# A graph-attention kernel's edge-list stage: two halves of a row searched as one, a mask by a square, and an order written by hand

## The chip, the cores and the metric

The kernel runs on one core of one Trainium2 chip. The metric is device time in microseconds of one execution. Five engines work side by side, each through its own queue in order: PE (matmul), DVE (vector), ACT (scalar, activations), POOL (GpSimd) and SP (which only issues DMAs here). They wait for each other through semaphores.

## The reference

4096 nodes carry 512 features each; `adj` is a 4096 x 4096 integer matrix, on average sparse, with denser rows and columns at low indices. The expected degree of row n and column j falls as 1/sqrt((n+1)(j+1)). Three attention layers run over the same edges, then two dense layers:

```python
h = jnp.einsum('nf,kfp->knp', node_matrix, W)
e = jax.nn.leaky_relu(f2[:, :, None] + f1[:, None, :], negative_slope=0.2)
e = jnp.where(adjacency_matrix[None, :, :] > 0, e, NEG_INF)
out = jnp.einsum('knm,kmp->knp', jax.nn.softmax(e, axis=-1), h)
...
x = _layernorm(x + layer0(x, adj))      # 8 heads of 64
x = _layernorm(x + layer1(x, adj))      # 8 heads, then 1 head of 512, then 512 -> 1024 -> 512
```

A row without edges takes the mean over all nodes. What matters here is that the edges of each row must be found once, as a list of source indices.

## The kernel before, in words

The kernel has a sparse path, whose result is used when all bounds of the lists hold, and a dense one, which is not entered with these inputs. The sparse path has a **graph stage** (`find_edges`, with `edge_constants` and `signs_of`), two head layers, and a last layer with the dense part. The head layers gather rows of a table of projected features by indirect DMA (L1094) with the lists of the graph stage. The change touches the graph stage and the functions beside it.

The graph stage goes through 32 tiles of 128 rows. Tile 0, the densest, is cut into four parts by columns; every other tile is one part, so that there are 35 parts (class `Part`). For a part:

- SP loads 128 x 4096 integers of `adj` (L846), ACT turns them into signs in bf16 (L848).
- **Keys.** For each 512 columns PE adds, in PSUM, the sign through an identity (L878) and a number that grows with the column (L879, `places` by `frac`). A column without an edge has a key below 1, a column with an edge 1 plus its place. Two windows of 1024 columns fit (`pk`, two buffers).
- **Maxima.** DVE takes the eight largest keys of each segment (`nc.vector.max`, L885). Segments are cut so that more than eight edges in one are very unlikely; tile 0 takes three rounds each, with `match_replace` (L888). The results lie side by side in `cand`.
- **List rounds.** DVE takes the k largest of `cand`, eight at a time (L900, L902), into `lst`.
- **Counts.** ACT turns the keys into column numbers `qs` (L907) and counts edges (L910); POOL makes the row's count (L912 to L929).
- **Place.** PE forms prefix sums over the rows (L933, `prs`); ACT reads them three times (L934, L939, L940), makes two Sign maps over the slots of the part (L944, L945), and POOL adds them (L946) into a matrix `s1` that says which slot belongs to which row. PE spreads the lists over slots (`pl`, L962 to L971, one buffer in PSUM), ACT copies the owner row of each slot (L973), DVE selects the one right entry of each slot (L979 to L983, or L988 for long lists), and POOL writes the index (L994 to L996).

`place` of a part is written into the program one part behind its maxima. Beside the parts, `beside(t)` projects tile t of x for the first layer: a load, four transposes on PE, eight small instructions on ACT (L686), eight matmuls (L697), copies (L710, L717) and the table's row store (L711). `load_projection` builds the three layers' weights with POOL products (L667) and DVE sums (L672, L677). The order on each engine's queue is chosen by the framework's scheduler in this stage; the later layers run under `tc.manual_schedule()`, that is in the order of the program.

At the end, some sums over the bounds make a flag. The first head layer clears seven gather buffers on ACT (L1307) and gathers.

Of the kernel before, what the change touches and what calls it, by code (L numbers as in the profile page):

```python
# [21 lines left out]
P = 128  # L22
# [23 lines left out]
GT = 4  # L46

# [23 lines left out]
class Part:  # L71
# [5 lines left out]
    def __init__(self, t, lo, hi, last):  # L77
# [3 lines left out]
        self.segs = []  # L81
        j = lo
        while j < hi:
            lim = min(hi, (j // 1024 + 1) * 1024)
            lam, k = 0.0, j
            while k < lim:
                more = lam + rate(top, k)
                if k - j >= 8 * r and tail(more, 8 * r) > 3e-7:
                    break
                lam, k = more, k + 1  # L90
            if 0 < lim - k < 8:
                k = lim - 8
            self.segs.append((j, k - j, r))
            j = k
# [464 lines left out]
def sparse_path(  # L559
# [32 lines left out]
    kmax = max(p.k for p in pts)  # L592
# [9 lines left out]
    nc.vector.tensor_copy(ident_b, ident)  # L602
    ones = const.tile([P, 1], F32, name="s_ones")
# [10 lines left out]
    for h in range(2):  # L614
        nc.gpsimd.memset(half[h * HN : (h + 1) * HN, h : h + 1], 0.5)
# [28 lines left out]
    def load_projection(pool, st, w, a):  # L644
# [15 lines left out]
        with tc.tile_pool(name=f"swload_{st.name}", bufs=2) as wp:  # L660
            for side in range(2):
                ab = wp.tile([P, hs, dm], F32, name="sab")
                nc.sync.dma_start(ab, a[:, ts(side, dm)].partition_broadcast(P))
                d = (side == 1) == st.dest_first
                for c in range(FC):
                    prod = wp.tile([P, 2, HF], F32, name="sprod")
                    nc.gpsimd.tensor_mul(  # L667
                        prod, st.w[:, c, :, :HF], ab.rearrange("p h d -> p (h d)").rearrange("p (j f) -> p j f", j=2)
                    )
                    if hs > 1:  # L670
                        at = HF if d else HF + hs // 2
                        nc.vector.tensor_reduce(  # L672
                            st.w[:, c, :, at : at + hs // 2],
                            prod.rearrange("p j (h d) -> p j h d", d=dm), AX.X, OP.add,
                        )
                    else:
                        nc.vector.tensor_reduce(st.w[:, c, int(d), HF:], prod, AX.XY, OP.add)  # L677
# [12 lines left out]

    def project_in(ps, st, columns, n=P):

        halves = []
        for j in range(2):
            ph = ps.tile([P, st.wide], F32, name="ph")
            for c in range(FC):
                nc.tensor.matmul(ph[:n], columns(c), st.w[:, c, j], start=(c == 0), stop=(c == FC - 1))  # L697
            halves.append(ph)
        return halves
# [35 lines left out]
    def project_mean(sb, ps, st):  # L735

        mean = sb.tile([P, FC], F32, name="mean")
        nc.vector.tensor_reduce(mean, st.xparts, AX.X, OP.add)
        nc.vector.tensor_scalar_mul(mean, mean, 1.0 / N)
        project_out(sb, st, project_in(ps, st, lambda c: mean[:, c : c + 1], 1), NT, 1)  # L740
# [32 lines left out]
    def edge_constants(big):  # L773
# [7 lines left out]
        places = big.tile([P, N // KW, P], BF16, name="places")  # L781
        nc.gpsimd.memset(places, 0.0)
        nc.gpsimd.memset(places[0:1], 64.0 / 8192)
        nc.gpsimd.memset(places[32:33], 1.0 / 8192)  # L784
        for w in range(1, N // KW):
            nc.gpsimd.memset(places[64:65, w], w * KW / 8192)
# [3 lines left out]
        iota_k = big.tile([P, longest, kmax], F32, name="iota_k")  # L790
        nc.gpsimd.iota(iota_k, [[-P, longest], [1, kmax]], base=0, channel_multiplier=0, allow_small_or_imprecise_dtypes=True)
# [23 lines left out]
        values = []  # L815
        for i, value in enumerate((-8192.0, 2.0**-14 - 1.0)):
            tile_ = big.tile([P, 1], F32, name=f"value{i}")
            nc.gpsimd.memset(tile_, value)
            values.append(tile_)
# [16 lines left out]
        mids = by_parts("mids", lambda p: 0.5 - p.chunks[1] * P, others, 0.5)  # L836
        ends_at = by_parts("ends_at", lambda p: -p.n * P, others, 0.0)
        return frac, places, iota_e, iota_k, row1, own_b, before, values, mids, ends_at, by_parts

    def signs_of(sb, t, pieces=1):  # L840

        raw = sb.tile([P, N], I32, name="raw", bufs=2)
        sg = sb.tile([P, N], BF16, name="sg")
        w = N // pieces
        for i in range(pieces):
            nc.sync.dma_start(raw[:, ts(i, w)], adj[ts(t, P), ts(i, w)])  # L846
        for i in range(pieces):
            nc.scalar.activation(sg[:, ts(i, w)], raw[:, ts(i, w)], AF.Sign)  # L848
        return sg

    def find_edges(big, sb, ps, pk, constants, sg, beside):

        frac, places, iota_e, iota_k, row1, own_b, before, (less, under), mids, ends_at, by_parts = constants
        nv = len(pts)
        over = big.tile([P, 4, nv], F32, name="over")
        degs = big.tile([P, nv], F32, name="degs")
        counts = big.tile([P, nv], F32, name="counts")
        starts = big.tile([P, nv], F32, name="starts")  # L860
# [3 lines left out]
        places_of = []  # L864
        for v, p in enumerate(pts):
            t, k, c0, nch = p.t, p.k, p.first, p.n
            if t > 0:
                sg = signs_of(sb, t)
            size = sum(8 * r for _, _, r in p.segs)
            cand = sb.tile([P, size], F32, name="cand", bufs=1 if t == 0 else 2, tag="cand0" if t == 0 else "cand")  # L870
            at = 0
            for w0_ in range(p.lo // 1024 * 1024, p.hi, 1024):
                a, b = max(w0_, p.lo), min(w0_ + 1024, p.hi)
                key = pk.tile([P, 1024], F32, name="key")
                for j in [a] + list(range((a // KW + 1) * KW, b, KW)):
                    e, w = min(b, (j // KW + 1) * KW), j // KW
                    out_ = key[:, j - w0_ : e - w0_]
                    nc.tensor.matmul(out_, ident_b, sg[:, j:e], start=True, stop=False)  # L878
                    nc.tensor.matmul(out_, places[:, w], frac[:, j - w * KW : e - w * KW], start=False, stop=True)  # L879
                for j, n, r in p.segs:  # L880
                    if not a <= j < b:
                        continue
                    part = key[:, j - w0_ : j - w0_ + n]
                    for i in range(r):
                        nc.vector.max(out=cand[:, at : at + 8], in_=part)  # L885
                        if i < r - 1:
                            left = sb.tile([P, 256], F32, name="left")[:, :n]
                            nc.vector.match_replace(  # L888
                                out=left, in_to_replace=cand[:, at : at + 8], in_values=part, imm_value=-1.0
                            )  # L890
                            part = left
                        at += 8

            r8 = 8 * p.segs[0][2]
            skip = sum(n <= r8 for _, n, _ in p.segs)
            last = cand.rearrange("p (s e) -> p s e", e=r8)[:, skip:, r8 - 1]
            nc.vector.tensor_reduce(over[:, 0, v : v + 1], last, AX.X, OP.max)
            lst = sb.tile([P, kmax], F32, name="lst")[:, :k]
            for i in range(k // 8):
                nc.vector.max(out=lst[:, ts(i, 8)], in_=cand)  # L900
                if i < k // 8 - 1:
                    nc.vector.match_replace(  # L902
                        out=cand, in_to_replace=lst[:, ts(i, 8)], in_values=cand, imm_value=-1.0
                    )

            qs = sb.tile([P, kmax + 1], F32, name="qs")[:, : k + 1]
            nc.scalar.activation(qs[:, :k], lst, AF.Identity, bias=less, scale=8192.0)  # L907
            signs = sb.tile([P, kmax], F32, name="signs")[:, :k]
            balance = sb.tile([P, 1], F32, name="balance")
            nc.scalar.activation(signs, lst, AF.Sign, bias=under, accum_out=balance)  # L910
            deg = degs[:, v : v + 1]
            nc.gpsimd.tensor_scalar(deg, balance, 0.5, k / 2, op0=OP.mult, op1=OP.add)  # L912
# [18 lines left out]
            def place(v=v, p=p, k=k, c0=c0, nch=nch, qs=qs, deg=deg):  # L931
# [21 lines left out]
                for h in range(2):  # L953
                    nc.scalar.activation(rhs[:, h, : k + 1], qs, AF.Copy, scale=half[:, h : h + 1])
# [4 lines left out]
                for lo in range(0, nch, per):  # L959
# [6 lines left out]
                    for block, groups, chunks in blocks_in(p, lo, m):  # L966
                        for of, w in ((rhs, k + 2), (rest, k + 1)):
                            if last:
                                nc.tensor.matmul(*last, start=False, stop=False)
# [30 lines left out]
            if len(places_of) > 1:  # L1000
                places_of.pop(0)()
# [629 lines left out]
```

## Time and profile before

| | us |
|---|---|
| runs: median of 3 (lowest to highest) | 2116.35 (2112.72 to 2120.27) |
| profiled execution, first to last instruction (span) | 2110.3 |
| graph stage in it: up to the first gather | 489.4 |
| first MAX8 on keys in it | 8.3 |

The profiled execution's own time is known as its span; the runs' times include what lies around it, and their median stands 6.05 us above the span.

A line of busy time by stretch gives the stretch, its length, then the busy time and instruction count of PE, PEld (weight loads, which overlap PE), DVE, ACT and POOL, then the granted TensorE clock as a share of full speed, the DMA engines' busy share and GB/s. A line of a group gives source line, engine, operation, output and inputs with their shapes, the count, busy time and the mean ns of one, then the engine's idle time just before and what ended it. A line of a wait gives who waited for whom, the total in us, the number of times and the longest.

### The profile page before, as it was taken

Reading aid. Unit: us, or ns where it says so; the run is one execution under the profiler, and the core shown is the slowest. Engines: PE = TensorE matmul, PEld = TensorE weight load, DVE = VectorE, ACT = ScalarE, POOL = GpSimd, SP = SyncE. Lnnn points to the kernel's source line nnn. Section 1 sums busy time; section 2 is a strip of 40 time slices with the busy share of each in tenths; the row PEclk is TensorE's granted clock in tenths of the full one; section 3 lists DMA queues with packets and bytes.
Section 4 is the critical chain, followed back from the end, with each engine's and each line's share of the span. In section 5 each row is a group of like instructions: output and inputs, shape, how many; then the busy total and the mean of one; then the engine's idle time right before and its main releaser. Section 6 shows DMA issues by size and latency. Waiting matters only on the chain.

```text
span 2110.3 us, 29302 instructions
## 1 busy us (share of the span) xinstructions
PE 1707.7 (81%) x8987; PEld 999.2 (47%) x8987; DVE 1323.1 (63%) x3933; ACT 663.4 (31%) x2316; POOL 1155.6 (55%) x1658
## 2 busy tenths in 40 slices
PE   4778777663888887848888988579999989998997
PEld 3555443221555565525555665354454444444444
DVE  6887777774899998947878878433433333433412
ACT  3447677664222222202333332121110212111111
POOL 5515444446777777737777777373647444443200
PEclk9899999775899999978999999889999999999999
DMA  7434566634777888737777777373546343534301
GB/s 230 150 101 161 210 259 226 224 145 131 231 234 230 252 238 241 208 87 195 185 189 191 194 200 192 123 223 91 158 119 185 110 127 91 156 103 122 97 13 47
DMA packets 132589, 351.94 MB, mean 167 GB/s; under 512 B 41922, under 2 KB 42954, under 8 KB 128454
## 3 DMA queue, kind: packets, MB, share of 16 engines
q0 software_dynamic: 74160, 206.25, 36.0%
q1 hardware_dynamic: 58262, 143.72, 19.3%
q8 instruction: 74, 1.21, 0.2%
q14 instruction: 93, 0.76, 0.1%
HBM read 347.31 MB, written 42.24 MB: 185 GB/s over the span
## 4 chain that ended last, share of the span: by engine, by line
PE 34%; DVE 19%; issue 15%; POOL 13%; DMA 12%; ACT 6%; SPq 1%; POOLq 0%; DVEq 0%; ACTq 0%
PE acc L1230 11%; PE p L1508 10%; DMA g<-table_t,idx 10%; POOL g L1094 9%; PE ph L697 5%; DVE g L1218 5%; PE p L1520 4%; DVE cand L885 2%; DMA xr<-sx_d 1%; DVE cand L902 1%; POOL s L946 1%; DVE lst L900 1%; ACT sides L945 1%; POOL sprod L667 1%; DVE sm L1197 1%
## 5 line engine op out<-in xcount | busy, mean ns | idle before, releaser
L1094 POOL DMA_INDIRECT g<-table_t,idx x927 | 941.1, 1015 | 552.9 <-issue 232.8
L1230 PE MATMUL acc<-g,sm 128*64 128x260 f32 (+2 forms) x4068 | 580.8, 415 | 175.1 <-DVE g L1218 141.8
L1230 PEld LDWEIGHTS acc<-g,sm 128*64 128x64 f32 x4068 | 328.3, 147 | 391.8 <-DVE g L1218 156.8
L697 PE MATMUL ph<-sw_t,xt 128*128 128x264 f32 (+1 forms) x1536 | 394.0, 404 | 51.5 <-ACT xt L686 51.3
L1218 DVE TENSOR_TENSOR g<-g,wp 128x2048 f32<-128x2048 f32 (+4 forms) x134 | 349.1, 2605 | 6.7 <-ACT wp L1173 6.7
L697 PEld LDWEIGHTS ph<-sw_t,xt 128*128 128x128 f32 x1536 | 291.9, 197 | 120.0 <-ACT xt L686 72.3
L885 DVE MAX8 cand<-key 128x8 f32<-128x353 f32 (+55 forms) x467 | 195.1, 445 | 74.6 <-PE key L879 74.4
L1508 PE MATMUL p<-sht,sl1w 128*128 128x512 f32 (+1 forms) x576 | 228.7, 553 | 0.7 <-DVE xr L1525 0.7
L1520 PE MATMUL p<-sl2w,shid 128*128 128x512 f32 x512 | 226.7, 597 | 0.0
L686 ACT ACTIVATE xt<-pt 128x128 f32<-128x128 f32 x384 | 101.3, 279 | 216.0 <-PE pt L683 215.8
L1508 PEld LDWEIGHTS p<-sht,sl1w 128*128 128x128 f32 x576 | 107.8, 191 | 111.5 <-issue 106.0
L1520 PEld LDWEIGHTS p<-sl2w,shid 128*128 128x128 f32 x512 | 95.2, 190 | 119.9 <-issue 119.4
L1165 DVE TENSOR_TENSOR z<-s,g 128x16 f32<-128x16 f32 (+9 forms) x294 | 46.6, 175 | 138.0 <-DMA g<-table_t,idx 134.9
L878 PE MATMUL key<-sg,s_identb 128*128 128x512 bf16 (+1 forms) x258 | 109.7, 426 | 20.6 <-DVE cand L885 11.1
L1511 ACT ACTIVATE shid<-p,sl1b 128x512 f32<-128x512 f32 (+1 forms) x72 | 46.1, 640 | 242.9 <-PE p L1508 242.9
L1267 DVE SCALAR_TENSOR_TENSOR o<-ex,o 128x512 f32<-128x512 f32 x64 | 44.2, 691 | 124.5 <-ACT ex L1266 124.3
L848 ACT ACTIVATE sg<-raw 128x4096 bf16<-128x4096 int32 (+1 forms) x39 | 116.9, 2996 | 8.9 <-PE key L878 5.2
L710 ACT COPY hrow<-ph 128x260 f32<-128x260 f32 (+2 forms) x194 | 71.0, 374 | 148.8 <-PE ph L697 148.4
L879 PE MATMUL key<-frac,places 128*128 128x512 bf16 (+1 forms) x258 | 109.4, 425 | 2.7 <-POOL places L784 2.7
L1205 DVE TENSOR_SCALAR sm<-iota_n,nl,w 128x64 f32<-128x64 f32 x339 | 83.8, 327 | 30.8 <-ACT w L1176 30.8
L1173 ACT ACTIVATE wp<-z 128x32 f32<-128x32 f32 (+4 forms) x134 | 27.5, 205 | 207.0 <-DVE g L1218 206.5
L1525 DVE TENSOR_TENSOR xr<-p,xr 128x512 f32<-128x512 f32 x32 | 22.0, 688 | 94.1 <-PE p L1520 93.6
(184 smaller groups left out, 1836.8 us busy)
## 6 DMA issues: line engine op xcount, KB each, us to landing
raw<-in_adj_dram SPq DMA_DIRECT2D x31, 2048.0 KB, 7.9
table_t<-hrow SPq DMA_DIRECT2D x64, 260.0 KB, 3.6
xr<-in_x_dram SPq DMA_DIRECT2D x64, 256.0 KB, 4.0
g<-table_t,idx POOLq DMA_INDIRECT x927, 3.8
table_t<-hrow SPq DMA_DIRECT2D x32, 257.0 KB, 4.3
sx_d<-o SPq DMA_DIRECT2D x32, 256.0 KB, 4.6
xr<-sx_d SPq DMA_DIRECT2D x32, 256.0 KB, 4.0
out_dram<-xr SPq DMA_DIRECT2D x32, 256.0 KB, 3.4
```

The source lines that it names most:

```text
L686: nc.scalar.activation(xt[:, c, :], pt[:, c, :], AF.Copy, accum_out=st.xparts[:, c, t : t + 1])
L697: nc.tensor.matmul(ph[:n], columns(c), st.w[:, c, j], start=(c == 0), stop=(c == FC - 1))
L848: nc.scalar.activation(sg[:, ts(i, w)], raw[:, ts(i, w)], AF.Sign)
L878: nc.tensor.matmul(out_, ident_b, sg[:, j:e], start=True, stop=False)
L879: nc.tensor.matmul(out_, places[:, w], frac[:, j - w * KW : e - w * KW], start=False, stop=True)
L885: nc.vector.max(out=cand[:, at : at + 8], in_=part)
L1094: nc.gpsimd.indirect_dma_start(out=u.g[:, k, : self.st.row], out_offset=None, in_=self.st.table[:, :], in_offset=bass.IndirectOffsetOnAxis ...
L1205: nc.vector.tensor_scalar(sm[:, at + i], of_g, node[k], u.w[:, k], op0=OP.is_equal, op1=OP.mult)
L1218: nc.vector.tensor_mul(body, body, wp[:, :, :, None].to_broadcast(body.shape))
L1230: nc.tensor.matmul(out_[g * HN : (g + 1) * HN], sm[:, slot], rows(k), start=start, stop=stop)
L1508: nc.tensor.matmul(p1, l1w[:, c, ts(k, P)], hts[b][:, c, :n], start=(c == 0), stop=(c == FC - 1))
L1520: nc.tensor.matmul(p2, hids[b][:, k, ts(j, P)], l2w[:, k, :], start=(k == 0), stop=(k == HC - 1))
```

## The change

Seven things are done at once.

- **Fold.** In tiles 1 to 31, columns c and c + 2048 share one key: PE adds half the sign of the first and the whole sign of the second, and a place with steps of 1/2048. The search runs over 2048 columns. If both columns have an edge, the key is above 2 and counts as one entry of the list; `MORE = 4` extra entries in front hold the first column of such doubles (key minus 2). Doubles sort first, so the extra entries come from the first four of the list.
- **Signs** come in halves of 2048 columns (`load`, `sign`), with a bias of -0.5.
- **Square.** `s1` is now 0 or 1: ACT squares twice the slot number plus an offset, (2e + middle)^2, in f32, and POOL compares it with the squared count.
- **Counts** have more small steps on ACT and POOL for the extra entries.
- **Order by hand.** A `Clock` adds up estimated DVE costs; steps are put into the program when their time has come (`later`), and projections of x when PE has room by the estimate (`idle`, `spare`). Parts are taken as one of tiles 31 to 8 first, then one of tiles 0 to 7 and two of the rest in turn.
- **List rounds between maxima.** A list's rounds and selections are generators; after each maximum one step of another list is put in. Two segments of tile 0 go in alternation.
- **Projection beside.** A transposed tile is copied by one ACT instruction; the sum of x for the mean row is built by POOL adds (`xsum`) in place of accumulated copies.

```diff
+        self.folds = t > 0
+        self.more = MORE if self.folds else 0
+        self.top = HW if self.folds else hi
...
+                more = lam + rate(top, k) + (rate(top, k + HW) if self.folds else 0.0)
...
+        def fill(i):
...
+                if pts[v].folds:
+                    ways = [(half_b, sgs[pts[v].t, 0]), (ident_b, sgs[pts[v].t, 1])]
+                    w += N // KW
+                else:
+                    ways = [(half_b, sgs[pts[v].t, j // HW])]
+                for i_, (of, sg) in enumerate(ways):
+                    nc.tensor.matmul(out_, of, sg[:, j % HW : j % HW + e - j], start=(i_ == 0), stop=False)
+                nc.tensor.matmul(out_, places[:, w], frac[:, j % KW : j % KW + e - j], start=False, stop=True)
...
+            if more:
+                nc.scalar.activation(lst[:, :more], lst[:, more : 2 * more], AF.Identity, bias=values["two"])
+            nc.scalar.activation(signs, lst, AF.Sign, bias=values["under"], accum_out=balance[:, 0:1])
...
-                sides = sb.tile([P, 2, most * P], BF16, name="sides")[:, :, :wide]
-                nc.scalar.activation(sides[:, 0], iota_e[:, :wide], AF.Sign, bias=first)
-                nc.scalar.activation(sides[:, 1], iota_e[:, :wide], AF.Sign, bias=ends[:, v : v + 1], scale=-1.0)
-                nc.gpsimd.tensor_add(here, sides[:, 0], sides[:, 1])
...
+            nc.scalar.activation(far, iota_e[:, :wide], AF.Square, bias=middles[:, v : v + 1], scale=2.0)
+            nc.gpsimd.tensor_scalar(here, far, lim[:, 1:2], None, op0=OP.is_lt)
...
-                for h in range(2):
-                    nc.scalar.activation(rhs[:, h, : k + 1], qs, AF.Copy, scale=half[:, h : h + 1])
+            nc.scalar.copy(rhs[:, :, : k + 1], q2)
...
+                clock.later(2.0 + 3.5e-3 * wide, queue, v, rhs, rest, lo, per)
...
+    class Clock:
+        def later(self, delay, fn, *args):
+            self.count += 1
+            heapq.heappush(self.due, (self.now + delay, self.count, fn, args))
+        def tick(self, cost):
+            end = self.now + cost
+            self.spare = min(self.spare + 1.2 * cost, 3.0)
...
+        turns_ = [light.pop(0)]
+        while heavy or light:
+            turns_ += heavy[:1] + light[:2]
+            heavy, light = heavy[1:], light[2:]
...
+            for cost in maxima(v, cand):
+                clock.tick(cost)
+                if side:
+                    step()
+            lists.append(v)
+            side.append(rounds(n, v, cand))
...
+            if t == 0:
+                nc.gpsimd.tensor_copy(xsum, xr)
+            else:
+                nc.gpsimd.tensor_add(xsum, xsum, xr)
```

In the changed program the search has 434 MAX8 on keys in place of 467, and the keys take 392 matmuls in place of 516. The code behind the graph stage is the same.

## The prediction

> **What bounds the kernel now.** I read the page's slices first, then the busy time by stretch, then the waits, then the last microseconds ahead of the first gather, then single rows for prices. From the page, in 40 slices of 52.8 us:
>
> ```profile
> PE   4778777663888887848888988579999989998997
> DVE  6887777774899998947878878433433333433412
> POOL 5515444446777777737777777373647444443200
> PEclk9899999775899999978999999889999999999999
> ```
>
> The change touches only the graph stage, the first nine slices and a bit. There no engine is full: PE and DVE show 6 to 8 tenths. The busy time by stretch gives the stage (0 to 489 us) and two parts of it; columns are PE, PEld, DVE, ACT, POOL, then clock, DMA share and GB/s:
>
> ```profile
> 0.00:489.00 489.00, 344.54 (x1747) 200.85 (x1748) 366.60 (x1415) 293.74 (x843) 214.50 (x731) 0.89 0.52 184
> 120.00:140.00 20.00, 18.51 (x94) 13.49 (x95) 15.13 (x90) 6.53 (x42) 3.87 (x17) 0.83 0.20 67
> 240.00:340.00 100.00, 74.84 (x417) 42.11 (x417) 76.23 (x250) 76.92 (x197) 43.55 (x158) 1.00 0.64 238
> 360.00:460.00 100.00, 66.16 (x277) 24.58 (x278) 72.38 (x219) 66.69 (x128) 43.16 (x172) 0.77 0.56 208
> ```
>
> DVE, the busiest, works 367 of 489 us; 122 us are waiting. So the stage is bound by order: four queues that each stop for another. The waits within the stage name the stops:
>
> ```profile
> DVE cand L885 <- PE key L879: 74.4, 55, 5.7
> POOL hole L974 <- ACT nl L973: 63.4, 28, 4.1
> PEld prs L933 <- POOL counts L927: 50.8, 31, 3.4
> PEld L969 <- POOL s L946: 48.3, 31, 2.7
> ```
>
> DVE waits 74 us for keys; PE, which makes the keys, stands at the prefix matmul and the list matmuls (50.8 and 48.3) for POOL. The stage's end is the last list's chain (timeline):
>
> ```profile
> 476.54 0.39 PEld L969 LDWEIGHTS <-s 128*128 128x128 bf16 x5 [1.39 <-POOL s L946]
> 485.20 0.17 ACT L973 COPY nl<-pl 128x5 f32<-128x5 f32 x1 [1.27 <-PE pl L971]
> 485.71 18.95 ACT L1307 ACTIVATE g<-s_ones 128x3120 f32<-128x3120 f32 x7 [0.34 <-DVE sel L979]
> 489.40 1.42 POOL L1094 DMA_INDIRECT g<-table_t,idx  x1 [2.49 <-PE pss L1126]
> ```
>
> The last MAX8 on keys ends at 477.2; lists, matmuls, copy, the first clearing of a gather buffer and the first gather follow in 12 us. Behind the gather 2110.3 - 489.4 = 1620.9 us remain, whose code the change leaves as it is.
>
> **The change, engine by engine.** Prices:
>
> ```profile
> L885 DVE MAX8 cand<-key 128x8 f32<-128x1024 f32 x6 | 7.4, 1230 | 3.0 <-PE key L879 3.0
> L885 DVE MAX8 cand<-key 128x8 f32<-128x78 f32 x4 | 0.9, 237 | 1.0 <-PE key L879 1.0
> L946 POOL TENSOR_TENSOR s<-sides 128x512 bf16<-128x512 bf16 (+7 forms) x35 | 50.3, 1437 | 35.6 <-ACT sides L945 32.3 <-ACT nl L973 3.4
> L945 ACT ACTIVATE sides<-iota_e,ends 128x512 bf16<-128x512 f32 (+7 forms) x35 | 29.2, 835 | 0.0
> L667 POOL TENSOR_TENSOR sprod<-sw_t,sab 128x512 f32<-128x512 f32 x24 | 29.0, 1241 | 8.2 <-DMA sab<-in_a_dram 4.6 <-DVE sw_t L677 1.5 <-DVE left L888 1.2
> ```
>
> *DVE.* A MAX8 costs (1230 - 237)/946 = 1.05 ns per column plus 155 ns, some 90 of which run under the next one. Today 32 tiles of 4096 columns are searched, 131,072 columns in 467 instructions. Folded, tiles 1 to 31 have 2048 columns: 4096 + 31 x 2048 = 67,584 in 434. That is 63,488 x 1.05 ns = 67 us less, and 1 to 2 us for 33 instructions. Candidate rows shrink from 4360 to 4096 entries in all (-2), the four extra entries widen each selection (+3), the second identity and a memset add 1. DVE falls from 367 to about 300. Tile 0's parts keep their three rounds. Putting list rounds between maxima I price at nothing: it fills gaps already counted as idle.
>
> *PE.* Of 516 key matmuls 392 remain: a folded window of 512 columns takes three in place of four. In the timeline they follow each other every 0.215 us at full clock and 0.43 at half, so 124 x 0.215 = 27 us, up to 53. The list matmuls stay (the extra entries add a few columns to each), as do the 32 projections. 344.5 - 27 = 317 at today's clock mix. The clock matters here: the rows above show 1.00 while PE still projects (240 to 340) and 0.77 after. A denser PE should sit nearer 1.00; I take a third of the gap of 11% back, 10 us: 307.
> [...]
>
> *ACT.* Two Sign maps become one Square: -29. The column copies of a transposed tile, eight instructions and 37 us in all, become one 128x512 copy, priced by sht<-pt in a later stage (584 ns): 32 x 0.58 = 19, so -18. Bands of rhs in one copy: -6; two of three prefix reads remain: -9. Added: 62 small steps on the extra entries (+16) and 31 more Sign instructions, since each tile comes in halves (+6). 294 falls to about 254.
>
> *POOL.* The add L946 goes (-50) and a compare of a squared distance (f32) comes, 23,168 columns in 35 instructions. No row shows a wide compare. Low end: the iota L788 writes 1536 columns in 1417 ns, 0.92 per column, 28 us with starts. High end: the compare-and-multiply of L974 grows from 247 ns at 4 columns to 300 at 12, 6.6 ns per column, 150 us. I take 50, L946 itself, because it has the same widths, place and output. Added: 32 adds of x at L667's 1.24 us (+40) and three more tiny steps a list, some 0.2 us each, with wider rests and constants (+28). 214.5 becomes 282, between 260 and 382.
> [...]
>
> *SP and transfers.* Halves double the adjacency DMAs to 62 of 1 MB; x loads, table stores and weights are issued in the same queue as before, and a load still stands behind whichever store waits for ACT. The stage moves 90 MB; in 366 us that is 246 GB/s, below the 259 of the best slice. I price it at nothing; if the cover goes, 90 MB at 238 (row above) take 378 us, 12 more.
>
> *Waits.* Each prefix and list matmul is now issued some planned microseconds behind its producers. If these delays hold, PE's stops for POOL (50.8 and 48.3) go; what is late next is PE itself, with 307 us of work for 300 of DVE. If they fail, the waiting matmul holds back the keys behind it on PE and DVE for those. Only one list tile in PSUM exists, and lists now queue for it.
>
> *Ends.* POOL's constants grow by some 2.3 us (places half as large again, seven more row fills of 0.15 to 0.5 us), so the first MAX8 moves from 8.3 to about 10.6. Projections need the summed weights, last reduced near 28 us today; I put their start at 35. The tail stays near 13.
>
> *Sum.* By 35 us PE has done about 10 us of its work, and about 4 lie in the tail: 293 us between. PE's busiest 20 us today are 18.51/20, 0.925; I take 0.92 as its share: 35 + 293/0.92 + 13 = 366. DVE's sum ends earlier (300/(366 - 24) is a share of 0.88). First gather at 366 instead of 489.4: -123. Span 2110.3 - 123 = 1987. The median of the runs stands 6 us above the profiled span: 1993.
>
> **The rivals.**
> *DVE-bound.* PE runs at full clock and never holds DVE: 10.6 + 300/0.95 + 12 = 338, time 1965. For it: 20 us with DVE full exist today. Against: PE's sum is no smaller than DVE's. Chance 0.13.
> *No denser than today.* Either hand order gives PE only the share of 240 to 340 (0.75): 35 + 293/0.75 + 13 = 439, time 2066; or POOL is the bound at its high end: 382/0.92 + 13 = 428, time 2055. For it: POOL stands in front of both PE waits. Against: the removed search makes every list come sooner. Chance 0.12.
> *Slower: the single list tile.* 50 list rounds pass through one PSUM buffer: matmuls (0.7 us), ACT's copy, perhaps behind a half-tile Sign of 1.9, then three DVE steps, each behind a maximum. I count 5 us, 250 in all, hidden. It decides from (489 - 48)/50 = 8.8 us a round; at 10 us the stage is 548 long and the time 2175. For it: the copy waits of 63 us above. Chance 0.04.
> *Nothing moves* because the stage's end hangs on something else, such as the table. Against: its last write is issued at 359.6 today, 130 us ahead of the first gather. Chance 0.02.
>
> **How the numbers follow.** The forecast has 0.69; its own range is 1955 to 2044, from 280 us of PE work at a share of 0.95 (35 + 266/0.95 + 13 = 328) to 317 at 0.82 (417). The range of 8 in 10 is 1950 to 2060: it takes in the DVE-bound case and the POOL end, and leaves out the slow tail of the no-denser case and the slower one. Faster by over 0.3% (6.3 us, about what a measurement of this kernel can tell from no change): 0.94; within: 0.02; slower: 0.04.
>
> **What would show it.** Right: MAX8 on keys near 130 us busy in place of 195; PE the busiest engine of the stage with a clock over 0.93; the waits of PE for POOL under 30 us; first gather between 340 and 400. Wrong: a compare row over 3 ns a column with POOL the fullest engine; DVE still waiting over 70 us for keys; or a change in the 1620.9 us behind the first gather, which I hold to be the same within 5.

## The result, and the profile after

The changed kernel takes 2139.78 us (median of 4 runs, 2136.9 to 2141.04), the kernel before, run beside it, 2114.79: a ratio of 1.0109, with a 95% interval of 1.0093 to 1.0125. It is slower by 1.1%, where 1993 us had been forecast. The profiled execution has a span of 2137.0 us; its first gather comes at 506.82, where 366 had been forecast and 489.40 was measured before.

```profile
506.82 1.35 POOL L1331 DMA_INDIRECT g<-table_t,idx  x1 [1.41 <-ACT g L1544]
```

The slices of the page show where: the graph stage now fills nine and a half slices of 53.4 us, and in it PE is no denser and its clock is lower than before.

```profile
PE   4777756662788888756887888679999989998997
PEclk8888878885899999988999999879999999999999
```

The busy time by stretch (stretch, length, PE, PEld, DVE, ACT, POOL, granted clock, DMA share, GB/s) of the part after the start, and of the tail behind the last MAX8 on keys:

```profile
35.00:480.00 445.00, 302.36 (x1537) 201.92 (x1535) 267.80 (x1269) 235.37 (x582) 258.98 (x690) 0.84 0.49 179
480.00:507.00 27.00, 6.96 (x71) 5.47 (x72) 9.41 (x37) 11.65 (x37) 19.34 (x65) 0.52 0.03 9
```

PE works 302 of 445 us, a share of 0.68; 0.92 had been assumed. No other engine is fuller there. Before, PE's share of the whole stage was 0.70 (344.54 of 489) and DVE's 0.75. So PE's and DVE's work did shrink, but the stage grew longer, and it holds more idle time than before. The waits of the stage (who for whom, total, times, longest) say for what:

```profile
ACT rhs L1049 <- POOL q L1048: 116.5, 35, 6.8
DVE sel L1101 <- ACT nl L1081: 96.4, 23, 12.5
PEld prs L1034 <- POOL counts L1005: 67.8, 20, 11.3
DVE cand L1142 <- PE key L973: 30.9, 8, 19.3
```

DVE's wait for keys has fallen (74.4 before), but in its place DVE stands 96 us at the first selection step of a list, waiting for ACT's copy of the owner row. ACT stands 116 us at the copy into rhs, a wait that the kernel before did not have. One list in the timeline shows how the two hang together (start, duration, engine, line, and in brackets the idle time before):

```profile
305.18 3.23 POOL L1042 TENSOR_SCALAR s<-far,lim 128x1152 bf16<-128x1152 f32 x1
308.39 0.33 POOL L1048 TENSOR_TENSOR q<-qs,half 128x90 f32<-128x90 f32 x1
308.75 0.27 ACT L1049 CAST rhs<-q 128x90 bf16<-128x90 f32 x1 [6.41 <-POOL q L1048]
...
313.72 0.24 ACT L1049 CAST rhs<-q 128x58 bf16<-128x58 f32 x1 [2.96 <-POOL q L1048]
313.87 0.16 ACT L1081 COPY nl<-pl 128x8 f32<-128x8 f32 x1
314.06 0.66 DVE L1101 TENSOR_TENSOR sel<-iota_k,pl 128x480 f32<-128x480 f32 x1 [1.85 <-ACT nl L1081]
...
316.37 0.59 PE L1034 MATMUL prs<-counts,before 128*128 128x1 f32 x2 [10.78 <-POOL counts L1005]
```

POOL writes the mask first (3.23 us) and only then the product q2 that ACT copies. ACT has waited 6.41 us, and 2.96 us more for the next list's product; all that is behind in ACT's queue has waited too, among it the copy nl (313.87). The signs from which POOL counts come late, so POOL's count comes late, and PE has stood 10.78 us at a prefix matmul with keys and projections queued behind it.

The theories from here: the hand order loses the time (E), above all through ACT behind POOL's compare (B) and through planned delays that are too short (C). Against it stand three others: that the late start (A) or the volume of POOL's work (D) costs it, or that the new work overlaps badly in whatever order (F).

### The profile page after: what moved, and what is told of

The parts are those of the page before. It is cut to its first block, busy times and chain, and to the rows that moved or that the text cites. A ratio compares the mean times of both kernels' runs of the same rounds, so it can differ in the third digit from the quotient of the medians.

```text
span 2137.0 us, 29108 instructions
## 1 busy us (share of the span) xinstructions
PE 1687.6 (79%) x8875; PEld 1011.4 (47%) x8875; DVE 1247.4 (58%) x3902; ACT 632.2 (30%) x2112; POOL 1241.6 (58%) x1794
## 3 DMA queue, kind: packets, MB, share of 16 engines
q1 hardware_dynamic: 62726, 143.72, 18.9%
## 4 chain that ended last, share of the span: by engine, by line
PE 33%; POOL 17%; issue 16%; DVE 15%; DMA 14%; ACT 5%; POOLq 0%; SPq 0%; DVEq 0%; ACTq 0%
DMA g<-table_t,idx 11%; PE p L1789 10%; PE acc L1467 10%; POOL g L1331 9%; PE ph L710 5%; PE p L1801 5%; DVE g L1455 5%; POOL s L1042 3%; DMA xr<-sx_d 1%; ACT sg L954 1%; DMA raw<-in_adj_dram 1%; DVE sm L1434 1%; PE key L972 1%; DVE bs L1508 1%; DVE cand L1142 1%
## 5 line engine op out<-in xcount | busy, mean ns | idle before, releaser
L710 PEld LDWEIGHTS ph<-sw_t,xt 128*128 128x128 f32 x1536 | 303.3, 202 | 117.3 <-ACT xt L701 36.1
L1142 DVE MAX8 cand<-key 128x8 f32<-128x48 f32 (+51 forms) x434 | 127.5, 314 | 31.2 <-PE key L973 30.9
L701 ACT ACTIVATE xt<-pt 128x128 f32<-128x128 f32 x256 | 67.4, 278 | 199.6 <-PE pt L698 199.6
L954 ACT ACTIVATE sg<-raw,value 128x2048 bf16<-128x2048 int32 x62 | 123.7, 2005 | 5.7 <-DMA raw<-in_adj_dram 5.5
L972 PE MATMUL key<-sg,s_halfb 128*128 128x512 bf16 x134 | 59.0, 441 | 56.8 <-DVE cand L1142 33.2
L1410 ACT ACTIVATE wp<-z 128x32 f32<-128x32 f32 (+4 forms) x134 | 27.5, 205 | 221.0 <-DVE g L1455 220.8
L1042 POOL TENSOR_SCALAR s<-far,lim 128x512 bf16<-128x512 f32 (+7 forms) x35 | 68.5, 1958 | 24.5 <-ACT far L1041 22.1
L1434 DVE TENSOR_TENSOR sm<-iota_n,nl 128x128 f32<-128x128 f32 (+4 forms) x266 | 75.0, 322 | 0.0
```

The costliest lines, as they stand in the source:

```text
L972: nc.tensor.matmul(out_, of, sg[:, j % HW : j % HW + e - j], start=(i_ == 0), stop=False)
L1042: nc.gpsimd.tensor_scalar(here, far, lim[:, 1:2], None, op0=OP.is_lt)
L1142: nc.vector.max(out=cand[:, at + 8 * q : at + 8 * q + 8], in_=part)
L1434: nc.vector.tensor_tensor(sm[:, at : at + n_], of_g[:, None, :].to_broadcast(shape), nl[:, c : c + n_, None].to_broadcast(shape), op=OP.is ...
```

## The experiments

Each kernel is the changed one with the edit shown. Runs e5 to e8 shared a chip that takes 2327.65 us for the kernel before; there 1834 to 1839 us lie behind the first gather in place of 1623 to 1633, while a MAX8 on keys has the same median (292 to 294 ns against 295), so these four are compared by the first gather, and by their time only as a ratio to before. Their times fell against before by nearly as much as their first gathers lie ahead of 489.4 (e5 89.6 and 88.5 us, e6 94.4 and 92.3, e7 30.5 and 29.0, e8 45.6 and 45.3), which speaks for a stage that runs as fast on that chip. Each first gather is read from one profiled execution; by the times, steps of up to some 8 us (e1, e3 against e2, e5, e6, e10 against e8) lie within overlapping intervals and are not shown to be real.

| run | first gather, us | time, ratio to before (95%) |
|---|---|---|
| changed kernel | 506.8 | 1.0109 (1.0093 to 1.0125) |
| e1, `values` first | 505.4 | 1.0100 (1.0078 to 1.0121) |
| e2, q2 ahead of the compare | 467.7 | 0.9895 (0.9869 to 0.9921) |
| e3, rhs straight from qs | 463.6 | 0.9882 (0.9864 to 0.9900) |
| e8, e3 with longer delays | 444.1 | 0.9804 (0.9773 to 0.9835) |
| e10, e8 with `values` first, compare on DVE | 437.2 | 0.9775 (0.9738 to 0.9812) |
| e11, e3 with rounds apart from maxima | 455.4 | 0.9808 (0.9775 to 0.9841) |
| e4, framework's order | 404.7 | 0.9618 (0.9592 to 0.9644) |
| e12, e4 with rounds apart | 417.9 | 0.9650 (0.9618 to 0.9683) |
| e7, e4 without the fold | 460.4 | 0.9865 (0.9842 to 0.9888) |
| e5, e4 with `values` first, rhs from qs | 400.9 | 0.9615 (0.9590 to 0.9641) |
| e6, e4 with the compare on DVE | 397.1 | 0.9592 (0.9564 to 0.9621) |
| e9, e5 and e6 together | 385.8 | 0.9502 (0.9470 to 0.9535) |

**The start.**

```diff
+        values = {} ... nc.gpsimd.memset(values[key], value)     # ahead of frac
         frac = big.tile([P, KW], BF16, name="frac")
...
-        values = {} ...                                          # behind `before`
```

> The changed kernel with one edit: the five small memsets of `values` (L854) come first among POOL's constants in place of near the end. In the changed kernel ACT's first Sign waits 16.2 us for them and starts at 18.25, the first MAX8 at 21.97 (before: 8.32). Theory A (the late start is lost in full): the first MAX8 comes at 9 to 13 us, and everything behind it moves with it, so that the first gather comes at 493 to 499 in place of 506.8 and the time falls by 8 to 13 us. Rival (the start is hidden, because the stage is bound by the lists' chains further on): first MAX8 early as well, but the first gather at 503 or later and the time within 4 us of the changed kernel.

The first MAX8 came at 12.2 in place of 22.0, and the first gather at 505.4: 1.4 us earlier, the rival. The lead is lost at the second tile, whose adjacency had not arrived; in the timeline of e1:

```profile
21.14 2.00 ACT L954 ACTIVATE sg<-raw,value 128x2048 bf16<-128x2048 int32 x1 [9.99 <-DMA raw<-in_adj_dram]
```

The median time is 5 us lower, but the ratios to before overlap; the profiled span is 8.7 lower, of which 7.3 lie behind the first gather, where both programs are the same, so that part is not the edit's.

**ACT behind POOL.**

```diff
# e2
-            nc.gpsimd.tensor_scalar(here, far, lim[:, 1:2], None, op0=OP.is_lt)
             nc.gpsimd.tensor_mul(q2, ...)
             nc.scalar.copy(rhs[:, :, : k + 1], q2)
             nc.gpsimd.tensor_copy(rhs[:, :, k + 1], row1)
+            nc.gpsimd.tensor_scalar(here, far, lim[:, 1:2], None, op0=OP.is_lt)
# e3
-            nc.scalar.copy(rhs[:, :, : k + 1], q2)
+            for h in range(2):
+                nc.scalar.activation(rhs[:, h, : k + 1], qs, AF.Copy, scale=half[:, h : h + 1])
```

> The changed kernel with one edit in `middle`: POOL makes q2 (L1048) and the owner column (L1050) before the wide compare (L1042) and not behind it; nothing else moves. In the changed kernel ACT's copy into rhs (L1049) waits 116.5 us for q2 in 35 waits, 3.3 us each; a compare takes 1.96 us of that. Theory B (ACT stands behind POOL, and what follows in ACT's queue is late for PE and for the selections on DVE): that wait falls to 35 to 60 us, DVE's wait for the owner copy nl (96.4 us) falls by 30 or more, and the first gather comes 25 to 60 us earlier (447 to 482). Rival C (the planned delays are too short for the chain ACT-POOL-PE-ACT whatever the order on POOL): the wait moves to the next link (list matmuls wait for s1, which is now later), and the first gather moves by less than 12 us. Rival D (the volume of POOL's work binds): no change at all, within 4 us.

> The changed kernel with one part of the change undone: rhs is copied straight from qs by two ACT instructions with the band's factor, as in the kernel before, so that ACT no longer waits for q2; POOL still makes q2 for rest, behind the compare. ACT gets 35 more small instructions, about 6 us. Theory B: the wait of 116.5 us is gone from ACT whole, DVE's wait for nl (96.4) falls by 40 or more, and the first gather comes 30 to 80 us earlier (427 to 477), more than with the edit that puts q2 first. Rival C (chain too long for the planned delays): less than 12 us, with PE's list matmuls now waiting for POOL's rest and s1. Rival D (POOL's volume): within 4 us.

Both are theory B: first gather at 467.7 and 463.6, and both beat the kernel before, by about 1%. In e2 ACT's wait for q2 fell from 116.5 to 49.2, DVE's for nl from 96.4 to 68.9 (a fall of 30 had been expected, 27.5 came). In e3 the wait for q2 is gone, at 10 us more work on ACT (rhs takes 19.0 us in place of 9.2); DVE's wait for nl stands at 65.0, so the second expectation of e3 (a fall of 40 or more) missed too. Taking the whole wait away brings only 4 us more than halving it, since other waits remain as they were, PE's at the prefix sum among them (58.8 in the changed kernel):

```profile
PE prs L1034 <- POOL counts L1005: 56.2, 18, 10.2
```

POOL's volume alone (D) is out: its busy time in e2 is that of the changed kernel (302 and 303 us), and the first gather still moved by 39 us.

**The order as a whole.**

```diff
-        pools.enter_context(tc.manual_schedule())
```

> The changed kernel without the order by hand: the line that sets the manual order for the pools of the graph stage is taken out, so that the framework's scheduler chooses each engine's order, as in the kernel before; fold, square, xsum and the program's text stay. Theory E (the hand order is what loses the time that the fold saves): with the density of the kernel before, where DVE, the busiest, worked 367 of 489 us (0.75), 318 us on PE and 289 on DVE would end at 318/0.75 = 424 plus start and tail, so the first gather comes at 400 to 450 and the time is 55 to 105 us below the changed kernel. Rival F (the work itself became harder to overlap: small chains through POOL for each list, whatever the order): first gather at 490 to 520, the time within 15 us of the changed kernel. Rival G (the scheduler does worse, because the generators write list rounds and maxima into the program in small pieces): first gather later than 520.

Theory E: 404.7, 102 us ahead of the changed kernel, with the same instructions. The stretch after the start, and the waits of the stage in e4:

```profile
35.00:382.00 347.00, 278.42 (x1548) 187.25 (x1546) 264.53 (x1282) 232.69 (x592) 251.18 (x695) 0.91 0.64 228
```

```profile
DVE sel L1101 <- ACT nl L1081: 51.2, 24, 6.4
PEld prs L1034 <- POOL counts L1005: 41.3, 18, 7.0
ACT rhs L1049 <- POOL q L1048: 28.4, 17, 7.7
```

The same three waits are there, each shorter. With the same instructions that means that the scheduler more often has other work of the same engine ahead of a step that is not ready. PE's share rises from 0.68 to 0.80 and the granted clock from 0.84 to 0.91.

**What the fold is worth.**

```diff
-        self.folds = t > 0
+        self.folds = False
...
-        nc.gpsimd.tensor_scalar(ends_at[:, folded:], ends_at[:, folded:], -MORE / 2, None, op0=OP.add)
```

> The framework's order and everything else of the change, with the fold undone: tiles 1 to 31 are searched over 4096 columns again, without the extra entries. DVE gets its 67 us of MAX8 back (287 to about 350), PE 27 to 35 us of matmuls, POOL and ACT lose some 20 us of small steps each. Theory N (the fold's saving is real once the order lets it through): first gather at 445 to 490 in place of 404.7, the time 40 to 85 us more. Rival O (the gain of the run with the framework's order came from the other parts, and DVE's search lay beside POOL's chains): first gather at 395 to 425.

Theory N: 460.4. Once the order lets it through, the fold is worth 55.7 us. The rest of the change with the framework's order (460.4 against the 489.4 of the kernel before) is worth 29, which was not divided further. DVE's work and PE's in e7:

```profile
0.00:460.00 460.00, 334.53 (x1726) 206.62 (x1754) 358.08 (x1417) 247.35 (x546) 279.09 (x773) 0.88 0.59 196
```

**The planned delays, and the repair of the hand order.**

```diff
# e8, on e3
-            clock.later(2.2, middle, v, qs, lim, off)
+            clock.later(5.0, middle, v, qs, lim, off)
-                clock.later(2.0 + 3.5e-3 * wide, queue, v, rhs, rest, lo, per)
+                clock.later(4.0 + 3.5e-3 * wide, queue, v, rhs, rest, lo, per)
# e10, on e8: `values` first as in e1, and
-            nc.gpsimd.tensor_scalar(here, far, lim[:, 1:2], None, op0=OP.is_lt)
+            nc.vector.tensor_scalar(here, far, lim[:, 1:2], None, op0=OP.is_lt)
```

> The hand order with rhs copied straight from qs (first gather 463.6 in that run), and two of the planner's delays made longer: 5.0 in place of 2.2 us of planned time between a list's last round and its prefix matmul, and 4.0 in place of 2.0 us (plus the part for the width) between that and its list matmuls. The selections' delay stays. The planner's own clock reads 269 us at the end of the lists where the chip needs 480, so a planned microsecond is about 1.7 real ones. Theory C (the steps are put in too early, and PE and DVE stand before them): PE's wait of the prefix matmul for the counts falls from 56 us to under 30 and the first gather comes at 415 to 450. Rival P (the delays do not matter: ACT and POOL take a list's steps in the order of their own queues, and a later place only moves the wait to DVE's selections): first gather at 455 to 475.

> The hand order repaired as far as single edits go: rhs straight from qs, the two longer delays, `values` first, and the wide compare on DVE (in the run with the longer delays, first gather 444.1, ACT's Square waited 29.2 us for POOL's compare, since `far` has one buffer). Theory C (the hand order loses by single late links, and each can be put right): first gather at 412 to 432. Rival U (no few constants can replace an order that follows estimated durations; the compare now stops DVE's maxima too): 436 to 460.

In e8 PE's wait at the prefix matmul fell from 56.2 to 5.9 us and the first gather came 19.5 us earlier, at 444.1: theory C, at the late end of its range. What stood longest there then, besides DVE's wait for nl (48.5) and PE's for free key windows (44.0); `far` holds ACT's squares:

```profile
ACT nl L1082 <- PE pl L1080: 51.7, 20, 7.1
ACT far L1041 <- POOL s L1042: 29.2, 11, 6.8
```

In e10 the second of these is gone and the first has grown to 62.6. DVE now stands for `far` instead, with the maxima behind it, and PE's wait for free key windows rises to 59.1. The first gather comes at 437.2: rival U.

```profile
DVE s L1042 <- ACT far L1041: 45.7, 21, 4.7
```

Each edit moved part of the stop to another engine of the same chain. e10 and e9 (below) have the same instructions and ran on one chip; only the order and its delays differ. 437.2 against 385.8 is 51 us that the repaired hand order still loses.

**List rounds between maxima.**

```diff
             side.append(rounds(n, v, cand))
+            while side:
+                step()
```

> The hand order with rhs straight from qs (first gather 463.6) and the list rounds not put between maxima: after a part's maxima its rounds and the selections that are due run to their end before the next part's maxima. Theory V (putting them between is a gain: PE makes the next keys meanwhile): first gather at 475 to 510. Rival W (a selection that stands in the middle of the maxima and waits for ACT is what holds DVE, so that apart is better): 430 to 458.

> The same edit (list rounds run to their end behind their part's maxima) under the framework's order, whose run had its first gather at 404.7. Theory X (the scheduler orders DVE by its own estimates, and the place in the program hardly counts): 395 to 415. Rival Y (the place counts there too, since PE's two key windows then stand full while DVE does rounds): 418 to 450.

Under the hand order apart is better by 8.2 us (455.4 against 463.6, rival W), with DVE's wait for nl at 35.0 in place of 65.0. Under the framework's order apart is worse by 13.2 (417.9), between the two ranges; DVE then waits 32.6 us for keys and 32.4 for kk (ACT's copy out of `pl` for the long lists), where e4 had 18.7 and 6.1, and 22.5 for nl where it had 51.2. By the ratios of the times the 8.2 us are nearer 16, in intervals that do not overlap, and the 13.2 nearer 7, in intervals that do. So this part of the change costs time in the order it came with; in the framework's order it looks like a gain, whose size is open.

**On the framework's order.** The edits of e5 are those of e1 and e3, that of e6 is the compare on DVE as in e10, and e9 has all three.

> The framework's order, and in addition the five `values` first among POOL's constants, and rhs copied straight from qs by two ACT instructions. In the run with the framework's order alone the first gather came at 404.7, the first MAX8 at 26.8 and ACT waited 28.4 us for q2. Theory J (ACT behind POOL still costs in this order): the wait of 28.4 goes and the first gather comes at 380 to 397. Rival K (the scheduler already puts other work into that wait, and the start is hidden as it was under the hand order): first gather at 399 to 410, the time within 6 us of that run.

> The framework's order, and in addition the wide compare (L1042) on DVE in place of POOL. In the run with the framework's order alone POOL is the fullest engine of the stage (299 of 404 us, PE 295, DVE 287). POOL loses 68 us of work; on DVE 23,168 columns at the 1.05 ns a column of a MAX8 and 35 starts would be 25 to 32 us. Theory L (POOL is what the lists wait for): the first gather comes at 370 to 393 in place of 404.7. Rival M (the compare now stops DVE's queue, because it waits for ACT's Square, and the maxima stand behind it): DVE has a wait of 20 us or more for `far`, and the first gather comes at 400 to 430.

> The framework's order with the three edits that each helped or did no harm: `values` first, rhs copied straight from qs, and the wide compare on DVE. Alone on that order the first two gave a first gather at 400.9 and the third at 397.1, where the order alone had 404.7. Theory Q (they shorten different links of a list's chain, ACT's and POOL's, and add up): first gather at 386 to 395. Rival T (they take away the same wait, or DVE's own queue is now what ends last): 396 to 406.

In e5 400.9 is rival K: the scheduler had hidden most of that wait. In e6 397.1 falls between the two expectations: POOL lost its 68 us, but DVE has a new wait of 27.5 us for `far`, and gives some of it back. Together they give 385.8, a little ahead of theory Q's range, and 18.9 us ahead of e4, where the two single gains were 3.8 and 7.6; e9 is clear of e4 by its time too. e9 takes 2014.72 us (2012.81 to 2020.63) against 2120.22 of the kernel before: a ratio of 0.9502. Its stage:

```profile
0.00:385.00 385.00, 284.56 (x1610) 190.54 (x1634) 306.78 (x1419) 264.18 (x673) 238.83 (x832) 0.92 0.68 234
```

## Why the prediction was wrong

**The step that failed** is in the sum: "I take 0.92 as its share" between 35 us and the tail, together with the sentence before it, "If these delays hold, PE's stops for POOL ... go". The share was 0.68. The best 20 us of the old order were taken for what a new order would reach on the whole; but in those 20 us ACT worked only 6.53 us and POOL 3.87, so the row could not show what their chains cost, and the order was never followed on these two engines. The same instructions in the framework's order come to 0.80, and the first gather to 404.7; so 102 of the 141 us between 366 and 506.8 are the hand order's. The other 39 go with an assumed share that no run reached: the highest, with three more edits, is e9's, about 0.82 (270.38 of 331 us).

Of the 147 us by which the time was missed, these 141 stand ahead of the first gather and 9 behind it; against that, the median lies 2.8 us above the profiled span and not 6.

Of the 102 us, the runs divide about 62: 43 go when ACT no longer waits for POOL's q2 (e3), 19.5 more with two longer delays (e8). About 39 remain between e8 and e4 (43 against e5, which copies rhs from qs as e8 does). Two more edits brought 7 (e10), and 51 remain to e9 with the same instructions; which places of the order hold them stays open.

**The wait I did not name.** "Bands of rhs in one copy: -6" counted two instructions becoming one. But the one reads q2, which POOL makes, where the two read qs, which ACT itself has made. The edit adds a wait of ACT for POOL behind the widest instruction on POOL, and under the hand order it cost 43 us of the stage to save 9 or 10 of ACT's busy time.

**Work, term by term**, predicted and measured in the stage: DVE 300 and 289.3, MAX8 on keys 130 and 127.5; ACT 254 and 261.7; PE 307 to 317 and 318.0; POOL 282 and 303.4. These held, PE's by luck, since two errors cancel there (see the clock below). Of the signs that were set out, the MAX8 near 130 and PE as the busiest engine came; the clock over 0.93, PE's waits for POOL under 30 and the first gather by 400 did not. POOL's main miss is the compare, 50 in the sum and 68.5 in the group's line:

```profile
L1042 POOL TENSOR_SCALAR s<-far,lim 128x512 bf16<-128x512 f32 (+7 forms) x35 | 68.5, 1958 | 24.5 <-ACT far L1041 22.1 <-PE pt L1643 1.6
```

From 1570 ns at 512 columns and 3218 at 1152 it is 2.6 ns a column, and the sum lies inside the bounds of 28 and 150 us. On DVE the same 35 take 24.3 us (e6):

```profile
L1042 DVE TENSOR_SCALAR s<-far,lim 128x512 bf16<-128x512 f32 (+7 forms) x35 | 24.3, 694 | 35.3 <-ACT far L1041 27.5 <-POOL qs L1021 4.1 <-ACT lst L985 1.5
```

**The clock.** A denser PE was to come near 1.00; it came to 0.83, and PE was no denser. Busy time multiplied by the clock estimates PE's work at full speed (in the changed kernel key matmuls follow each other every 0.215 us at 304 us, at a clock of 1.00, and every 0.43 at 318 us, at 0.50): 344.54 x 0.89 = 307 before, 317.96 x 0.83 = 264 after, 284.56 x 0.92 = 262 in e9. So this work fell by about 43 us, more than the 27 priced, and a slower clock gave part of it back: busy time fell by only 27. The 16 us beyond the price were not traced to a line. No run shows the 280 us of PE work at which the prediction's own range begins: PE was busy for 317.96 us in the changed kernel and 284.56 in e9, at clocks of 0.83 and 0.92, and by the products above its work was 262 to 264. In the stop of 10.78 us in the timeline above, idle time was followed by a slower clock: the granted clock is 1.00 until 310.1, 4.5 us into the stop, then 0.50 from 310.2 to 320.4. The prefix matmul at 316.37 takes 0.59 us, where the ones at 299.84 and 303.17, at a clock of 1.00, take 0.38.

**Start and tail.** The first MAX8 came at 22.0, not 10.6, because `values` stands near the end of POOL's constants and the Sign now has a bias from it; I had counted POOL's time and not who waits for which constant. It was worth 1.4 us (e1). The tail was 26.8 us (480.0 to 506.8), not 13, since the last lists, which all pass through ACT and POOL, end one behind the other: PE waits 13.5 of these us for POOL's counts, at three prefix sums. In e9 the tail is 17.

**The rivals.** "No denser than today", in its first form, was the right mechanism. Its price was too kind: it took the old share, 0.75, as the floor, and so ended at 2066 on the side of a gain. The slow rival, the single list tile, is not what happened: PE waits 10 us in all for selections before it may overwrite `pl`. DMA at nothing held (e9 moves the same bytes at a busy share of 0.68).

**Behind the first gather** 1630.2 us remained where I had allowed 5 around 1620.9. The eight runs on chips like the first, with the same code there, lie between 1622.9 (e1) and 1633.1 (e9): these profiles differ by more than I allowed, and one profile of before cannot say whether the few us above it are real.

## What to carry to other kernels

An order written by hand is a claim about every engine's queue at once: follow one item through the smallest engines' queues, and look at each instruction that now reads another engine's result, before taking a saving in work as a saving in time. Where a scheduler is at hand, run the same program under both orders; here that one line was worth 102 us, and the interleaving, a loss of 8 us under the hand order, was no loss under the scheduler and by the first gather a gain of 13. Here, when one late link was put right, another engine of the chain became the stop, and the repair by single edits ended 51 us short of the scheduler's order.

## What the runs showed of the hardware that was not expected

The wide compare costs POOL 2.6 ns a column (f32 in, bf16 out) and 68.5 us in all, and DVE 24.3 us: a factor of 2.8 for the same 35 instructions. And the clock differed between the two orders: with the same instructions, between 35 us and the last MAX8 on keys, the granted clock was 0.84 in the one order and 0.91 in the other, and PE's busy time 302 and 278 us. The product of the two is nearly the same, 254 and 253 us.
